# A GNN-attention-expert layer: the order of the expert routing, the distance of the second expert layer, and the last two tiles

## The chip, the cores and the metric

The kernel runs on one core of a Trainium2 chip. A core has a matrix engine (PE, with a separate queue for loading weights, PEld), a vector engine (DVE), a scalar engine (ACT), a general engine (POOL) and a queue engine (SP) that mostly starts DMA transfers. Each engine works through its own instructions in order and waits for the others by semaphores; ACT, SP and POOL also start transfers between the chip's memory (DRAM) and the on-chip memory. The metric is the device time of one execution in microseconds (us).

## The reference

One layer of a graph network over 1250 rows of 768 columns, in float32. A graph attention with two stages and a linear-attention mixer are added to `x`. What the change touches is the last part, a mixture of experts:

```python
logits = flat @ router_w.T                       # 1250 x 8
probs = jax.nn.softmax(logits, axis=-1)
topk_probs, topk_idx = jax.lax.top_k(probs, 2)
importance = probs.sum(axis=0)
running = 1 + 0.1 * (importance - 1) + 0.01
balanced = topk_probs / running[topk_idx]
balanced = balanced / balanced.sum(axis=-1, keepdims=True)
h = silu(einsum('th,eih->tei', flat, w1))        # 8 experts, 256 hidden
outs = einsum('tei,ehi->teh', h, w2)
x = x + sum over the two chosen experts of balanced * outs
```

`flat` is the normalised row. Each row thus goes to two of eight experts and gets back a weighted sum of two results.

## The kernel before

The rows are cut into ten tiles of 125 (`P`). The first 850 us hold the graph attention and the mixer and are not changed. The first five tiles of the updated rows are finished while the second attention layer of the other five still runs (`first_half`, L1131); there `stored` (L945) writes each finished row with its mean and reciprocal deviation (770 columns, `DX`) to two places in DRAM, `x2_d` and `xh_d`. The other five tiles are finished in the loop at L1242, and `stored(1)` writes them to `x2_d`.

**Expert tiles.** The kernel multiplies only what is chosen. It sorts the 2500 pairs of row and expert into tiles of 125 pairs that share one expert. The first 8 tiles, one for each expert, are filled from the first half of the rows and read `xh_d`; 16 more (`NQ1` = 24 in all) hold the rest and read `x2_d`. If the choice is uneven, a branch at the end computes up to nine further tiles; with these inputs it is not taken.

**Routing.** `placed` (L1048) ranks the logits, marks the two best and counts with two matmuls where each pair goes. `routed` (L1355) is a generator. Each call of `next(rt)` emits one portion of small DVE instructions and at times a list matmul on PE. A list is made by multiplying one-hot rows (`oh_r`) with values in bfloat16 pieces: `tokens` (L1301) makes the lists of row numbers, `roles` (L1323) the shares (weights), and for each pair the place of the row's other pair. The buffer `big` (5 x 770 columns) holds the one-hots during routing and gathered rows afterwards.

**The main loop** (L1478) has one step for each k from 0 to 23. For expert tile q:

- `gather(q)` (L1167) is an indirect DMA on POOL into one of 18 row buffers (`room`).
- `normed(q)` (L1176) normalises it, on ACT for the first eight tiles and on DVE for the others.
- `turned(q)` (L1189) transposes it on PE, and ACT copies it out of PSUM.
- `products(q)` (L1199) is the first expert layer, `gated(q)` (L1218) the silu, `hidden_turned(q)` (L1225) the transposition of the result.
- `halved(q)` (L1435) is the second expert layer: eight matmuls into `po`, then ACT scales by the share into `y`, SP stores `y` to `y_d` in DRAM and DVE adds it to the gathered row.
- `fetch_half(q)` (L1456) gathers by indirect DMA, for each pair of tile q, the result of the row's other pair if that one stands in an earlier tile. `hand_out(q)` (L1464) adds this half on DVE and scatters the finished rows to the output by another indirect DMA.

A row is written out by the later of its two tiles; for all others the index is out of bounds and the transfer leaves them out. All orders on PE, DVE, ACT and POOL are written out by hand here (`manual_schedule`), so each of these engines works in the order of the code. SP's order comes from a scheduler. Step k emits in this order:

```python
gated(k); turned(k + 2); next(rt, 0)
# one or two of halved(done), in part here and in part after products
normed(k + 3); products(k + 1); hidden_turned(k)
# POOL: hand_out(given), fetch_half(asked), then gather(got)
```

The constants at L1156 are `AHEAD` = 6 (how far gathers run ahead), `BEHIND` = 3 (buffers for fetched halves) and `LAG` = 6 (the first step with a `halved`). From step 6 on up to two `halved` go into a step, until the second layer is one tile behind the first; that is so from step 12 on. After the loop `halved(23)`, the remaining fetches and the remaining `hand_out` follow, each in turn.

Of the kernel before, what the change touches and what calls it, by code (L numbers as in the profile page):

```python
# [19 lines left out]
D = 768  # L20
# [49 lines left out]
def kernel(  # L70
# [874 lines left out]
    def stored(hf):  # L945

        t0, t1 = hf * TH_, (hf + 1) * TH_
        rs3 = rs3s[hf] = rstd_of(small, mv3, "c", t0, t1)
        nc.vector.tensor_copy(acc[:, t0:t1, D : D + 1], mv3[:, t0:t1, 0:1])
        nc.vector.tensor_copy(acc[:, t0:t1, D + 1 : DX], rs3.unsqueeze(2))  # L950
        for t in range(t0, t1):
            nc.sync.dma_start(out=x2_t[:, t, :], in_=acc[:, t, :DX])
            if not hf:
                nc.sync.dma_start(out=xh_t[:, t, :], in_=acc[:, t, :DX])
# [93 lines left out]
    def placed(psum, hf, pl):  # L1048
# [24 lines left out]
        pcum = psum.tile([P, 2, TH_, NE], F32, tag="rt" if hf else "tr", name=f"pcum_{hf}", bufs=1)  # L1073
# [12 lines left out]
        nc.vector.tensor_tensor(pos[:, hs], pcum[:, 0], cum, ALU.add)  # L1086
        picked(0, hs, pos[:, hs].unsqueeze(2).to_broadcast([P, TH_, 2, NE]), pick)
# [15 lines left out]

    def first_tiles(psum):
# [6 lines left out]
        pick0 = rtc.tile(two0, F32, name="pick0")  # L1111
# [44 lines left out]
    AHEAD, BEHIND, LAG = 6, 3, 6  # L1156
# [7 lines left out]
    room += [acc[:, t, :DX] for t in range(TH_, NT)] + [big[:, i * DX : (i + 1) * DX] for i in range(5)]  # L1164
    assert len(room) == 18
# [59 lines left out]
    def hidden_turned(q):  # L1225
        hT = exa.tile([128, 2, P], F32, tag="hT", name=f"hT_{q}", bufs=LAG + 1)

        def keep_h(b0, n, pt):
            if q < NE:
                nc.scalar.copy(hT, pt[:, :n, :])  # L1230
            else:
                nc.vector.tensor_copy(hT, pt[:, :n, :])  # L1232

        transposed(ps_x, hws.pop(q), [(0, 128), (128, 128)], keep_h, f"he{q}", bufs=3)
        hts[q] = hT
# [4 lines left out]
    plg = ps_x.tile([P, TH_, NE], F32, tag="rt", name="plg")  # L1240
    ft = first_tiles(ps_x)
    for i in range(TH_ + 3):  # L1242
# [8 lines left out]
        if 1 <= i <= TH_:  # L1251
            updated(ps_x, TH_ + i - 1)
# [22 lines left out]
    halves = exb.tile([P, BEHIND, D], F32, name="halves")  # L1275
    nc.gpsimd.memset(halves, 0.0)
# [24 lines left out]
    def tokens(oh, q0, q1):  # L1301
# [6 lines left out]
        plist = ps_x.tile([P, 2, w], F32, tag="rt", name=f"plist_{q0}")  # L1308
# [13 lines left out]

    def roles(oh, q0, q1, o, n):  # L1323


        w = q1 - q0
        more = carved(o, n * 2, 6, w)
        for i in range(3):
            listed(more[:, :, i, :], oh, parts[i][:, :n])
        listed(more[:, :, 3, :], oh, later[:, :n])  # L1330
        for i, v in ((4, q_), (5, r_)):
            for k in range(2):
# [3 lines left out]
                )  # L1336
        yield
        pmore = ps_x.tile([P, 6, w], F32, tag="rt", name=f"pmore_{q0}")
        for i in range(n * 2):
            nc.tensor.matmul(pmore, oh_r[:, i, :], more[:, i], start=(i == 0), stop=(i == n * 2 - 1))  # L1340
        lists = rtc.tile([P, 6, w], F32, tag="lists", name=f"lists_{q0}")
        nc.vector.tensor_copy(lists, pmore)
        nc.vector.tensor_tensor(share[:, q0:q1], lists[:, 1, :], lists[:, 2, :], ALU.add)
        nc.vector.tensor_tensor(share[:, q0:q1], share[:, q0:q1], lists[:, 0, :], ALU.add)
        goal = rtc.tile([P, 2, w], F32, tag="goal", name=f"goal_{q0}")
        nc.vector.scalar_tensor_tensor(
            goal[:, 0, :], lists[:, 4, :], float(P), lists[:, 5, :], op0=ALU.mult, op1=ALU.add
# [3 lines left out]
            goal, goal, -BIG, lists[:, 3:4, :].to_broadcast([P, 2, w]), op0=ALU.add, op1=ALU.mult  # L1351
        )
        nc.vector.tensor_scalar(take[:, 1:3, q0:q1], goal, BIG, None, op0=ALU.add)

    def routed():  # L1355


        pl = placed(ps_x, 1, plg)
        next(pl)
        yield  # L1360
        for _ in pl:
# [11 lines left out]
        nc.vector.tensor_tensor(q_[:, TH_:], nth[:, TH_:], at[:, 1, TH_:], ALU.add)  # L1373
        rows_of(1)
# [6 lines left out]

        def each(v):
            return v.unsqueeze(2).to_broadcast([P, NT, NE])

        nc.vector.tensor_reduce(red[:, 1, :], prob, AX.X, ALU.add)
        nc.vector.reciprocal(red[:, 2, :], red[:, 1, :])
        nc.vector.tensor_tensor(prob, prob, each(red[:, 2, :]), ALU.mult)

        imp = rtc.tile([P, NE], F32, name="imp")
        nc.vector.tensor_reduce(imp, prob.rearrange("p t e -> p e t"), AX.X, ALU.add)  # L1390
# [3 lines left out]
        pim = ps_x.tile([P, NE], F32, tag="rt", name="pim")  # L1394
        nc.tensor.matmul(pim, ones[:P, :P], imp, start=True, stop=True)
        nc.vector.tensor_scalar(used, end[0:1, NE - 1 : NE], 1.0, None, op0=ALU.add)

# [4 lines left out]
        run = rtc.tile([P, NE], F32, name="run")  # L1402
        nc.vector.tensor_scalar(run, pim, 1.0, 1.0 - 0.9, op0=ALU.subtract, op1=ALU.mult)
        nc.vector.tensor_scalar(run, run, 1.0, 0.01, op0=ALU.add, op1=ALU.add)
        rrun = rtc.tile([P, NE], F32, name="rrun")
        nc.vector.reciprocal(rrun, run)
        nc.vector.tensor_tensor(prob, prob, rrun.unsqueeze(1).to_broadcast([P, NT, NE]), ALU.mult)
        yield
        comb = lg
        nc.vector.tensor_tensor(comb, sel, prob, ALU.mult)  # L1410
        nc.vector.tensor_reduce(red[:, 3, :], comb, AX.X, ALU.add)
        nc.vector.reciprocal(red[:, 3, :], red[:, 3, :])
        nc.vector.tensor_tensor(comb, comb, each(red[:, 3, :]), ALU.mult)
        picked(2, slice(0, NT), comb.unsqueeze(2).to_broadcast(two), pick)

        rest = at[:, 2]
        for i in range(3):
            nc.vector.tensor_copy(parts[i], rest)
            if i < 2:
                nxt = rtc.tile([P, NT, 2], F32, name=f"rest_{i}")  # L1420
                nc.vector.tensor_tensor(nxt, rest, parts[i], ALU.subtract)
                rest = nxt
        yield
        oh_a = carved(6180, TH_, 2, NE)
        told(oh_a, 0, NE)
        first_ones = roles(oh_a, 0, NE, 2500, TH_)
        next(first_ones)
        yield
        for _ in first_ones:
            pass  # L1430
        yield
        for _ in roles(oh_b, NE, NQ1, 2980, NT):
            yield

    def halved(q, keep=True):  # L1435
# [17 lines left out]
        nc.vector.tensor_tensor(xg[:, :D], xg[:, :D], y, ALU.add)  # L1453
        sums[q] = xg[:, :D]

    def fetch_half(q):  # L1456
        if q > 0:
            nc.gpsimd.indirect_dma_start(  # L1458
                out=halves[:, q % BEHIND, :], out_offset=None, in_=y_d[0 : q * P, :],
                in_offset=bass.IndirectOffsetOnAxis(ap=take[:, 1, q : q + 1], axis=0),  # L1460
                bounds_check=q * P - 1, oob_is_err=False,
            )

    def hand_out(q):  # L1464
        fin = sums.pop(q)
        if q > 0:
            nc.vector.tensor_tensor(fin, fin, halves[:, q % BEHIND, :], ALU.add)
# [10 lines left out]
    for k in range(NQ1):  # L1478
        gated(k)
        if k + 2 < NQ1:  # L1480
            turned(k + 2)
        next(rt, 0)
        n = min(2, k - done) if k >= LAG else 0
        if k == NQ1 - 1:
            n = 1
# [3 lines left out]
        if k + 3 < NQ1:  # L1489
            normed(k + 3)  # L1490
        if k + 1 < NQ1:
            products(k + 1)
# [3 lines left out]
        hidden_turned(k)  # L1496
        while asked < done - 1:
# [5 lines left out]
        if given == 0 < done:  # L1503
# [3 lines left out]
        while k >= 3 and got < min(given + len(room), k + 1 + AHEAD, NQ1 if k >= 8 else len(room) - 5):  # L1507
            gather(got)
            got += 1
    halved(NQ1 - 1, keep=False)  # L1510
    assert done == NQ1 - 1
# [80 lines left out]
```

## Time and profile before

| | us |
|---|---|
| median of 3 runs | 1088.83 (1085.12 to 1092.47) |
| the profiled execution | 1084.71 |
| its span | 1082.9 |
| PE busy | 989.9 (91%) |
| DVE busy | 646.6 (60%) |
| ACT busy | 388.2 (36%) |
| POOL busy | 159.9 (15%) |
| first expert product starts | 884.4 |
| last matmul ends | 1055.2 |

The span is the time from the first to the last instruction of the profiled execution. Rows of the profile name the line of the code, the operation, the output and its inputs, and the duration. `ph` is the output of `products`, `po` that of `halved`, `tr_xe` that of `turned`, `tr_he` that of `hidden_turned`. `x_d` is `x2_d`. [...] In square brackets stands the idle time of the engine before the row, and what ended it.

### The profile page before, as it was taken

To read this page: it belongs to the slowest core of one execution; us is meant where nothing else is said; L and a number is where in the kernel's file an instruction comes from. 1 tells how busy PE (TensorE), PEld (TensorE's weight loads), DVE (VectorE), ACT (ScalarE), POOL (GpSimd) and SP (SyncE) were. 2 spreads that over 40 slices of the span, in tenths; PEclk is the share of its full clock that TensorE was granted. 3 is DMA by queue.
4 is the path that set the end of the run, shared out by engine and by line. 5 is a ranking of instruction groups with operands and counts; after the bars stand their busy time and mean duration, and the time that the engine had idled before them with its cause. 6 is when DMAs were issued, how large, how long until landed. Compare 5 with 4: busy or idle time off the path is not lost. (4 is left out here: it accounts for less than half of the span.)

```text
span 1082.9 us, 13295 instructions
## 1 busy us (share of the span) xinstructions
PE 989.9 (91%) x4893; PEld 754.6 (70%) x4893; DVE 646.6 (60%) x1411; ACT 388.2 (36%) x697; POOL 159.9 (15%) x157
## 2 busy tenths in 40 slices
PE   5988999999997999999999999999999788999980
PEld 4877888874574558989889875567778577766750
DVE  7338974441845835776675984946677655444542
ACT  0244422330000007646556750045457344332320
POOL 1000000000000000000000011432210031256543
PEclk9998999999998999999999999999999899999995
DMA  8400000031232101000002232221062268255443
GB/s 209 139 29 4 16 23 22 13 111 71 75 118 91 54 24 42 15 24 24 24 23 89 84 131 96 86 75 52 25 212 85 97 197 271 85 167 176 149 119 101
DMA packets 55429, 93.26 MB, mean 86 GB/s; under 512 B 22705, under 2 KB 29041, under 8 KB 55355
## 3 DMA queue, kind: packets, MB, share of 16 engines
q1 hardware_dynamic: 30966, 73.63, 20.0%
q0 software_dynamic: 15904, 17.02, 5.7%
q10 hardware_dynamic: 8484, 1.65, 0.8%
q8 instruction: 43, 0.70, 0.3%
q14 instruction: 32, 0.25, 0.1%
HBM read 75.53 MB, written 27.04 MB: 95 GB/s over the span
## 5 line engine op out<-in xcount | busy, mean ns | idle before, releaser
L777 PE MATMUL pa_a<-acc,p_a 125*125 125x197 f32 x800 | 144.6, 333 | 1.1 <-DVE p_a L773 0.7
L777 PEld LDWEIGHTS pa_a<-acc,p_a 125*125 125x125 f32 x800 | 133.7, 187 | 12.6 <-issue 5.8
L773 DVE SCALAR_TENSOR_TENSOR p_a<-e_a,cntT 125x625 f32<-125x625 f32 x80 | 64.5, 816 | 40.9 <-PE pa_a L777 39.8
L642 PE MATMUL pg<-W,xnT 128*125 128x396 f32 x240 | 82.5, 507 | 6.0 <-DVE acc L645 6.0
L337 DVE TENSOR_SCALAR ohd<-iota,dst_f 125x125 bf16<-125x125 int16 (+1 forms) x170 | 50.5, 297 | 61.4 <-PE pe L344 61.4
L849 PE MATMUL po<-wu_sb,xnT 128*125 128x384 f32 x240 | 82.0, 490 | 5.4 <-ACT acc L853 4.1
L483 PE MATMUL pk_k<-xnT,wk_sb 128*128 128x250 f32 x360 | 83.2, 374 | 0.0
L483 PE MATMUL pk_q<-xnT,wq_sb 128*128 128x250 f32 x360 | 80.0, 375 | 2.7 <-PEq L695 1.9
L771 DVE SCALAR_TENSOR_TENSOR e_a<-e_a,e_a 125x625 f32<-125x625 f32 x80 | 65.9, 835 | 25.6 <-ACT e_a L767 13.9
L483 PEld LDWEIGHTS pk_q<-xnT,wq_sb 128*128 128x128 f32 x360 | 67.2, 189 | 12.0 <-issue 3.3
L769 ACT ACTIVATE e_a<-rowt_a,s1x 125x625 f32<-125x625 f32 x80 | 64.5, 817 | 30.7 <-DVE e_a L771 30.5
L642 PEld LDWEIGHTS pg<-W,xnT 128*125 128x125 f32 x240 | 45.9, 192 | 42.0 <-DVE acc L645 6.7
L767 ACT ACTIVATE e_a<-rowt_a,s 125x625 f32<-125x625 f32 x80 | 64.6, 815 | 28.4 <-DVE p_a L773 27.0
L1441 PE MATMUL po<-ew,hT 128*125 (+1 forms) x192 | 68.7, 502 | 5.5 <-DVE hT L1232 5.0
L483 PEld LDWEIGHTS pk_k<-xnT,wk_sb 128*128 128x128 f32 x360 | 66.9, 189 | 6.8
L459 DVE CUSTOM_DVE_ANT_0 junk<-nmr,rows 125x1250 f32<-125x1250 bf16 x40 | 58.3, 1457 | 19.9 <-DMA rows<-sr_d 14.4
L1212 PE MATMUL ph<-ew,xTe 128*125 (+1 forms) x288 | 69.3, 392 | 0.0
L849 PEld LDWEIGHTS po<-wu_sb,xnT 128*125 128x125 f32 x240 | 43.6, 188 | 36.0 <-ACT acc L853 6.7
L333 DVE TENSOR_SCALAR ohs<-iota,smod,wgt 125x417 bf16<-125x417 int16 x170 | 65.4, 385 | 0.0
L1212 PEld LDWEIGHTS ph<-ew,xTe 128*125 128x125 f32 x288 | 55.6, 195 | 12.0
L344 PE MATMUL pe<-ohs,ohd 125*125 125x418 bf16 x206 | 55.4, 369 | 9.2 <-DVE ohd L337 8.5
L777 PEld LDWEIGHTS pa_b<-h,p_b 125*125 125x125 f32 x400 | 49.2, 193 | 8.7 <-DVE p_b L773 2.8
(344 smaller groups left out, 1591.0 us busy)
## 6 DMA issues: line engine op xcount, KB each, us to landing
y_d<-y SPq DMA_DIRECT2D x23, 375.0 KB
ew<-in_w1T SPq DMA_DIRECT2D x8, 768.0 KB
ew<-in_w2T SPq DMA_DIRECT2D x8, 768.0 KB
nmr<-nm_d SPq DMA_DIRECT2D x20, 305.2 KB
rowt_a<-ab_d SPq DMA_DIRECT2D x8, 610.4 KB
x_d<-acc SPq DMA_DIRECT2D x10, 376.0 KB
acc<-in_x SPq DMA_DIRECT2D x10, 375.0 KB
xr<-in_x SPq DMA_DIRECT2D x10, 375.0 KB
```

The lines of the kernel that those rows point to most:

```text
L333: nc.vector.tensor_scalar(oh_s[:, :TH], iota[:, :TH], smod[:, c : c + 1], wgt[:, c : c + 1], op0=ALU.is_equal, op1=ALU.mult)
L459: nc.vector.tensor_tensor_reduce(out=junk, in0=nm, in1=row, scale=1.0, scalar=-3.0e38, op0=ALU.add, op1=ALU.max, accum_out=mx_col)
L483: nc.tensor.matmul(pk[:, i, :], w_sb[:, k, f * 128 : (f + 1) * 128], xnT[:, k, g * GN : (g + 1) * GN], start=(k == 0), stop=(k == KD - 1),)
L642: nc.tensor.matmul(pg, xnT[:, k, t * P : (t + 1) * P], W12[:, k, cs], start=(k == 0), stop=(k == KD - 1))
L767: nc.scalar.activation(e1, rowt[:, 0, :], AF.Exp, bias=s[:, h, 0, u : u + 1])
L769: nc.scalar.activation(e2, rowt[:, 1, :], AF.Exp, bias=sx[:, h, u : u + 1])
L771: nc.vector.scalar_tensor_tensor(e1, e1, 1.0, e2, op0=ALU.min, op1=ALU.max)
L773: nc.vector.scalar_tensor_tensor(p, e1, 1.0, cntT[:, u, hf * HN : (hf + 1) * HN], op0=ALU.min, op1=ALU.mult)
L777: nc.tensor.matmul(pas[i][:, :cw], p[:, i * P : (i + 1) * P], hv, start=(u == 0), stop=(u == NT - 1))
L849: nc.tensor.matmul(po[:, hf, :384], xnT[:, k, ts], wu_sb[:, k, cs], start=(k == 0), stop=False)
L1212: nc.tensor.matmul(ph, xT[:, k, :], ew1[:, whose_r[q], k, :].rearrange("p o i -> p (o i)"), start=(k == 0), stop=(k == KD - 1),)
L1441: nc.tensor.matmul(po[:, hf, :384], hT[:, c, :], ew2[:, e_r, c, hf * 384 : (hf + 1) * 384].rearrange("p o n -> p (o n)"), start=(c == 0), ...
```

## The change

**Stores.** In the first half all stores to `xh_d` go ahead of those to `x2_d`. In the second half each tile's 768 columns are stored when the tile is done, and mean and deviation of all five tiles follow in one transfer of two columns.

**Routing.** The balanced weights are computed ahead of the lists. A new `first_shares` makes the shares of the first eight tiles from `pick0`, directly after. Two portions of `routed` are emitted in each step, one before and one after the matmuls. All small PSUM results share one bank, `prt`, each at its own columns. `roles` makes three lists for the first tiles instead of six. The routing ends in step 6 and not in step 8.

**Loop.** `LAG` is 3, so `halved` starts in step 3 and is one tile behind from step 6 on. The tiles under 8 are normalised ahead of the routing portion. Fetches start at step 7 and have six buffers, two of them parts of `big`; `room` has 16. Gathers of tiles 8 to 12 start at step 4, those from 13 on at step 9 (before: 3 and 8).

**Last two tiles.** Fetches for tiles 22 and 23 read only the results of tiles 0 to 20. For a row whose other pair stands in tile 21 or 22, a one-hot matrix (`chosen`, in steps 10 to 12) picks the result from SBUF by a matmul (`crossed`). The last `halved` adds with one DVE instruction from PSUM.

The core of the diff:

```diff
-        for t in range(t0, t1):
-            nc.sync.dma_start(out=x2_t[:, t, :], in_=acc[:, t, :DX])
-            if not hf:
-                nc.sync.dma_start(out=xh_t[:, t, :], in_=acc[:, t, :DX])
+        if hf:
+            nc.sync.dma_start(out=x2_t[:, t0:t1, D:DX], in_=acc[:, t0:t1, D:DX])
+        else:
+            for to in (xh_t, x2_t):
+                for t in range(t0, t1):
+                    nc.sync.dma_start(out=to[:, t, :], in_=acc[:, t, :DX])
...
-    AHEAD, BEHIND, LAG = 6, 3, 6
+    AHEAD, BEHIND, LAG = 6, 6, 3
+    LATE = 2
...
-            updated(ps_x, TH_ + i - 1)
+            t = TH_ + i - 1
+            updated(ps_x, t)
+            nc.sync.dma_start(out=x2_t[:, t, :D], in_=acc[:, t, :D])
...
+    halves = [halves_t[:, i, :] for i in range(BEHIND - 2)]
+    halves[2:2] = [big[:, i * DX : i * DX + D] for i in (3, 4)]
+    PAIRS = [(q, f) for q in range(NQ1 - LATE, NQ1) for f in range(NQ1 - LATE - 1, q)]
...
+    def first_shares():
+        more = carved(6340, TH_ * 2, 3, NE)
+        for i in range(3):
+            listed(more[:, :, i, :], pick0, parts[i][:, :TH_])
+        yield
+        psh = prt[:, 136:160].rearrange("p (i q) -> p i q", i=3)
+        for i in range(TH_ * 2):
+            nc.tensor.matmul(psh, oh_r[:, i, :], more[:, i], start=(i == 0), stop=(i == TH_ * 2 - 1))
+        three_l = rtc.tile([P, 3, NE], F32, name="three_l")
+        nc.vector.tensor_copy(three_l, psh)
+        nc.vector.tensor_tensor(share[:, :NE], three_l[:, 1, :], three_l[:, 2, :], ALU.add)
+        nc.vector.tensor_tensor(share[:, :NE], share[:, :NE], three_l[:, 0, :], ALU.add)
...
+    def chosen(j):
+        oh = exa.tile([P, P], F32, tag="chosen", name=f"chosen_{j}", bufs=1)
+        nc.vector.tensor_scalar(oh, col, which[:, j : j + 1], None, op0=ALU.is_equal)
+        pt = ps_x.tile([128, 4, P], F32, tag="tr", name=f"tr_ch{j}", bufs=3)
+        nc.tensor.transpose(pt[:P, 0, :], oh, ident[:P, :P])
+        nc.scalar.copy(chosenT[:, j, :], pt[:P, 0, :])
+
+    def crossed(q):
+        fs = [(j, f) for j, (q2, f) in enumerate(PAIRS) if q2 == q]
+        for hf in range(2):
+            px = ps_x.tile([128, 4, P], F32, tag="tr", name=f"px_{q}_{hf}", bufs=3)
+            px = px.rearrange("p a b -> p (a b)")[:P, :384]
+            for n, (j, f) in enumerate(fs):
+                nc.tensor.matmul(
+                    px, chosenT[:, j, :], kept[f][:, hf * 384 : (hf + 1) * 384],
+                    start=(n == 0), stop=(n == len(fs) - 1),
+                )
+            cs = slice(hf * 384, (hf + 1) * 384)
+            to = (sums[q] if q in sums else xgs[q])[:, cs]
+            nc.vector.tensor_tensor(to, to, px, ALU.add)
...
-        nc.vector.tensor_tensor(xg[:, :D], xg[:, :D], y, ALU.add)
+        if keep:
+            nc.vector.tensor_tensor(xg[:, :D], xg[:, :D], y, ALU.add)
+        else:
+            xa = xg[:, :D].rearrange("p (a c) -> p a c", a=2)
+            nc.vector.scalar_tensor_tensor(
+                xa, po[:, :, :384], share[:, q : q + 1], xa, op0=ALU.mult, op1=ALU.add
+            )
...
-    for k in range(NQ1):
+    LISTS, ROLES = 4, 7
+    for k in range(NQ1 - 1):
         gated(k)
         if k + 2 < NQ1:
             turned(k + 2)
+        if k + 3 < NE:
+            normed(k + 3)
         next(rt, 0)
         n = min(2, k - done) if k >= LAG else 0
-        if k == NQ1 - 1:
-            n = 1
         if n and k > LAG:
             halved(done)
             done, n = done + 1, n - 1
-        if k + 3 < NQ1:
+        if NE <= k + 3 < NQ1:
             normed(k + 3)
-        if k + 1 < NQ1:
-            products(k + 1)
+        if k == NQ1 - 2:
+            hidden_turned(k)
+            halved(done)
+            done += 1
+        products(k + 1)
         if n:
             halved(done)
             done += 1
-        hidden_turned(k)
-        while asked < done - 1:
+        next(rt, 0)
+        if k != NQ1 - 2:
+            hidden_turned(k)
+        if 10 <= k < 10 + len(PAIRS):
+            chosen(k - 10)
+        while k >= ROLES and asked < min(done - 1, NQ1 - LATE - 1):
             if asked - given == BEHIND:
                 hand_out(given)
                 given += 1
             fetch_half(asked)
             asked += 1
-        if given == 0 < done:
+        while k >= ROLES and (given == 0 < done or (k > NQ1 - 6 and given < asked - 2)):
             hand_out(given)
             given += 1
-        while k >= 3 and got < min(given + len(room), k + 1 + AHEAD, NQ1 if k >= 8 else len(room) - 5):
+        while k >= LISTS and got < min(given + len(room), k + 1 + AHEAD, NQ1 if k >= 9 else len(room) - 3):
             gather(got)
             got += 1
-    halved(NQ1 - 1, keep=False)
-    assert done == NQ1 - 1
+    while asked - given > 2:
+        hand_out(given)
+        given += 1
+    nc.gpsimd.memset(halves_t[:, 2:4, :], 0.0)
+    for q in range(asked, NQ1):
+        fetch_half(q)
+    q = NQ1 - 1
+    gated(q)
+    crossed(q - 1)
+    hand_out(given)
+    hidden_turned(q)
+    crossed(q)
+    hand_out(given + 1)
+    halved(q, keep=False)
+    given += 2
     while given < NQ1:
-        if asked < NQ1 and asked - given < BEHIND:
-            fetch_half(asked)
-            asked += 1
-        if asked < NQ1 and asked - given < BEHIND:
-            continue
         final = hand_out(given)
         given += 1
```

## The prediction

> **What bounds the kernel now.** I read the page first, then the busy time by stage, then the order of single instructions in the expert stage, then the chain that ended last. All that the change touches begins near 858 us, and nearly all of it after 884 us, where the first expert tile is multiplied. Two rows of the page are used below (the second, for ACT's queue: packets, MB, share of 16 engines' span):
>
> ```profile
> span 1082.9 us, 13295 instructions
> ...
> q10 hardware_dynamic: 8484, 1.65, 0.8%
> ```
>
> The stages after 884 us (length, then the busy time of PE, PEld, DVE, ACT, POOL, granted clock, DMA share, GB/s):
>
> ```profile
> 884.00:954.00 70.00, 64.02 (x330) 49.83 (x329) 33.96 (x121) 28.77 (x57) 14.04 (x11) 0.95 0.58 182
> 972.00:990.00 18.00, 14.51 (x60) 9.96 (x59) 8.26 (x13) 5.07 (x10) 13.14 (x10) 0.91 0.65 192
> 990.00:1040.00 50.00, 49.28 (x222) 36.14 (x221) 24.98 (x39) 16.67 (x31) 28.79 (x21) 1.00 0.46 142
> 1055.20:1082.90 27.70, 0.00 (x0) 0.00 (x0) 5.67 (x6) 0.90 (x1) 9.78 (x8) 0.54 0.35 103
> ```
>
> From 990 to 1040 PE has 49.28 of 50 us: the steady steps are PE's. In the 70 us of the ramp (routing and the first tiles) PE idles 6 us, in 972 to 990 it idles 3.5, and after 1055.2 it has nothing for 27.7 us. One steady step of the loop, from the order of instructions, PE and then POOL:
>
> ```profile
> 1027.45 0.38 PE L146 MATMUL tr_he<-ident,hw 125*128 125x125 f32 x2
> 1027.69 0.83 PE L146 MATMUL tr_xe<-ident,xme 125*128 125x125 f32 x6
> 1028.43 2.82 PE L1441 MATMUL po<-ew,hT 128*125 x8
> 1031.08 2.75 PE L1212 MATMUL ph<-ew,xTe 128*125 x12
> 1033.67 0.38 PE L146 MATMUL tr_he<-ident,hw 125*128 125x125 f32 x2
> ```
>
> ```profile
> 1029.47 1.23 POOL L1468 DMA_INDIRECT out<-big,take  x1 [3.42 <-DVE big L1467]
> 1031.00 1.29 POOL L1458 DMA_INDIRECT halves<-y_d,take  x1 [0.30 <-issue]
> ```
>
> A step is the hidden transposes `he(k)` (`hidden_turned`), `turned(k+3)`, `halved(k)`, `products(k+2)`; the next `he` is at 1033.67, so 6.22 us, with no idle of PE. On POOL the `out` goes 2.02 us after `he`, for its DVE add stands behind the copy of `he`; the fetch of a half goes at 3.55 and the next gather at 5.1 (1020.14 after the `he` of 1015.00). POOL at the end:
>
> ```profile
> 1061.42 1.23 POOL L1468 DMA_INDIRECT out<-acc,take  x1 [0.30 <-issue]
> 1062.95 1.38 POOL L1458 DMA_INDIRECT halves<-y_d,take  x1 [0.30 <-issue]
> 1064.64 1.23 POOL L1468 DMA_INDIRECT out<-acc,take  x1 [0.30 <-issue]
> 1067.77 1.22 POOL L1468 DMA_INDIRECT out<-acc,take  x1 [1.91 <-DVE acc L1467]
> 1071.51 1.20 POOL L1468 DMA_INDIRECT out<-spare,take  x1 [2.52 <-DVE spare L1467]
> ```
>
> After the last product POOL and the landings are the chain: `out`, fetch, 7.2 us to land, an add on DVE of 0.96 at 1070.26, the last `out`, and 11.4 us from its issue to 1082.9.
>
> **The change, part by part.** I follow `he(k)`, the end of step k.
>
> *Ramp, steps 0 to 6.* The new order is one tile behind from step 6 on; before it is so only from step 12. The `normed` of the first tiles now precedes the routing on DVE, which takes away ACT's late normalisations: PE waited 7.9 us for them in five places (the waits of this stage); three of the five, 1.78 + 2.15 + 1.45 = 5.4 us, go. In their place come waits of PE for lists. In three slots the list's matmuls stand directly behind `turned`, and the DVE work that they need was queued behind an add that waits for the last `halved`. Take step 4: po ends, ACT's `y` 0.15 + 0.90, the add 0.96, the comparison and two lists 1.43 (900.76 to 902.19), in all 3.5 us; beside it PE has only `he` and `turned`, 0.87. So 2.6 us there, 2.6 at step 5 by the same sum, and 2.3 at step 2, where the shares' list waits for DVE (its chain from 889.28, with the rows of before: 899.7; PE is there at 897.4). PE's work from 884.37 to `he(6)`: the first product 4.05, seven at 2.6, seven `turned` at 0.64, seven `he` at 0.22, six `halved` at 2.6 (start to start in the chain), list matmuls 4.3 (0.38 + 0.53 + 0.54 + 1.13 + 0.54 + 1.14 in before): 48.1 us; with 7.5 us for lists and 1.4 in small waits `he(6)` is at 941.4. Three steps on, `he(9)` is at 960.0 with 9 halves done; `he(11)` would be at 972.5 with 11. Before has `he(11)` at 971.54 with 11. The ramp thus gives nothing: +1.0. The second-layer weights load in time: their first use is near 906 and not 922.9, but 1.9 MB of stores no longer stand ahead of them (882.05 to 887.2).
>
> *Stores.* Five stores of whole rows become five of 768 columns, earlier, and one of two columns: 625 runs of 8 bytes. The nearest row is ACT's queue of small packets: 0.8% of 16 engines' 1083 us over 8484 packets is 16 ns each, so 625 take 10 us of one engine. [...]
>
> *Gathers.* This is the term that decides. Tile 13 is gathered in step 9 (`k >= 9`; before in step 8), and in POOL's order it stands behind `hand_out(1)` and `fetch_half(7)`. The `out` of tile 1 waits for a DVE add behind the copy of `he(9)`. So POOL stands idle for some 10 us and gather 13 issues at `he(9)` + 5.1 = 965.1. Gathers of that place took:
>
> ```profile
> L1170 POOL DMA_INDIRECT big<-x_d,take x5: 1214/1227/1883, 946.7 to 984.1; - x5
> ...
> DMA to landing us min/median/max: 7.9/10.4/12.5
> ```
>
> With 10 us it lands at 975.1. `normed(13)` is on DVE in step 10, ahead of the copy of `he(10)` and the new comparison of `chosen(0)`: 0.7 + 0.4 + 0.2, then PE has one transpose and `turned(13)` at 976.8, where it was due at 966.5 (`he(10)` + 0.24). Queued behind on DVE: the copy, the comparison, `out(2)`; on PE: everything. +10.3; ends: 8 with a landing of 7.9, 13 with 12.5. From then on gather k+6 leaves at `he(k)` + 5.1 and is wanted at `he(k+3)`, as before.
>
> *Clock.* After a gap the clock can be low:
>
> ```profile
> 899.91 0.86 PE L146 MATMUL tr_xe<-ident,xme 125*128 125x125 f32 x6 [2.15 <-ACT xme L1182]
> 900.61 4.44 PE L1212 MATMUL ph<-ew,xTe 128*125 128x256 f32 x12
> ```
>
> This product took 4.44 us behind a 2.15 us gap; at full clock 2.76. [...] But 2.24 us of idle at 1050 to 1052 left the next po at 2.82, so I take +1.7.
>
> *Steady steps 11 to 21.* Before lost 6.2 us there against 10 x 6.22, 5.5 of it in 972 to 990, where adds waited for halves fetched late. With six halves in flight this goes: -6.2. `chosen` adds two more PE transposes with their order, +0.5; five adds at step 19 (4.8 us of DVE) delay `normed(23)` by about 1.1. So `he(21)`: 976.8 + 6.0 + 1.7 + 62.2 + 0.5 + 1.1 = 1048.3; before 1039.90.
>
> *End.* From `he(21)` the order po(21), `he(22)`, po(22) is what before does one step later: po(22) ends at +9.07, the tile's add at +11.0, `out(18)` at +12.2. Then a memset of 1536 columns (1.4, from 2.04 for 2304), three fetches at +15.2, +16.8, +18.4 (1.29 and 0.30 each), landing 7.2, add 1.0, `out` at +26.85, 11.4 to the end: +38.25. Before: 1082.9 - 1039.9 = 43.0. The matmuls of `crossed` (six of 0.7 us) and po(23) end at +19.3 and the last fused sum at +20.4: hidden under the landing; without that cover they would cost 4.2. Gain 4.75.
>
> *Sum.* 1048.3 + 38.25 = 1086.5 against a span of 1082.9: +3.6 us. The profiled execution took 1084.71; the median of the runs is 1088.83 (1085.12 to 1092.47), so 1092.
>
> **Rivals.** *Gathers in time*: if POOL reaches gather 13 a step earlier, or `out(1)` does not hold it, the 10.3 and 1.7 go: -8.4, 1080. For it: before has the same gathers go straight behind a fetch (946.67). Against: in the steady step every `out` waits for its add. *Cold clock*: all three list gaps pay 1.7 each and the gathers land in 13 us, as at 994.5 to 1007.8: 3.6 + 5.1 + 3 = +11.7, 1100.5, slower. It decides from three cold gaps on; with one it stays within 1%. *The end on PE*: if the three last fetches land before po(23) ends, DVE goes straight from the fused sum (+20.4) through three adds (2.9) to the last `out` (+23.5) and the end is at +34.9 instead of +38.25: 1089. Against: they leave at +15.2 to +18.4, and none of before landed in under 6 us.
>
> **How the numbers follow.** A measurement of this kernel tells about 1% (11 us) from no change. The forecast, with the end on PE in it, 0.55 (1085 to 1099); gathers in time 0.19 (1074 to 1085); cold clock or another late transfer 0.26 (1097 to 1110). The range from 1077 leaves out about 0.08 below and to 1104 about 0.1 above. Faster by over 1% needs the gathers in time and 2.5 us more: 0.14; slower takes most of the cold case and a little of the forecast: 0.26.
>
> **What would show it.** PE idle in one piece of 8 to 13 us near 966 to 977, ended by tile 13's normalisation, POOL idle before `out(1)`; list matmuls waiting 2 to 3 us at steps 2, 4, 5; no losses from 980 to 1040; after the last matmul about 19 us, ended by the fetch of tile 23. Wrong would be: no piece over 3 us after `he(9)`; the lists' DVE work faster than my queue sums; or a second late transfer.

## The result: 1% slower than before

The changed kernel took 1098.9 us in the median (1096.55 to 1103.24, 8 runs), the kernel before 1090.05 (1085.12 to 1098.81, 8 runs beside it). The ratio is 1.011, with a 95% interval of 1.008 to 1.014. The ratios, here and below, leave out single runs over 1.5% above the fastest of their kernel and need not equal the quotient of the medians (1.008 here). The prediction was 1092, about no change, in a range of 1077 to 1104. The time lies in the range; the kernel is slower by about 1%, and the interval leaves out no change.

The profiled execution of the changed kernel has a span of 1096.0 us against 1082.9. A row of its page, and the first gather that reads `x2_d`:

```profile
span 1096.0 us, 13377 instructions
...
917.55 1.23 POOL L1178 DMA_INDIRECT acc<-x_d,take  x1 [38.31 <-DVE used L1467]
```

This gather was released by DVE's routing (`used`) and not by the 625 short stores. The stages of the changed kernel (length, then the busy time of PE, PEld, DVE, ACT, POOL, granted clock, DMA share, GB/s):

```profile
888.00:951.00 63.00, 56.07 (x294) 43.26 (x293) 32.13 (x120) 26.74 (x50) 12.09 (x10) 0.95 0.55 177
951.00:969.00 18.00, 18.00 (x83) 13.27 (x82) 6.87 (x12) 6.56 (x13) 6.20 (x6) 1.00 0.35 112
969.00:987.00 18.00, 6.67 (x21) 4.49 (x21) 2.67 (x6) 1.40 (x4) 7.42 (x6) 0.62 0.39 109
1002.00:1052.00 50.00, 49.49 (x225) 36.38 (x224) 28.62 (x44) 16.77 (x33) 32.08 (x23) 1.00 0.51 152
1074.50:1096.00 21.50, 0.03 (x1) 0.00 (x0) 3.89 (x4) 0.90 (x1) 8.08 (x7) 0.59 0.33 93
```

The ramp (888 to 951) is idle on PE for 6.9 of 63 us. From 951 to 969 PE has no gap at all. From 969 to 987 it works for 6.7 of 18 us, and that stretch was not in the kernel before. The steady steps are as full as before (49.49 of 50), and from 1074.5 on PE is done for 21.5 us. Steps of the loop look as they did, PE first and then POOL, from the order of instructions:

```profile
1022.74 0.38 PE L146 MATMUL tr_he<-ident,hw 125*128 125x125 f32 x2
...
1028.96 0.38 PE L146 MATMUL tr_he<-ident,hw 125*128 125x125 f32 x2
```

```profile
1024.74 1.23 POOL L1548 DMA_INDIRECT out<-acc,take  x1 [1.42 <-DVE acc L1547]
```

A step is still 6.22 us, from `he` at 1022.74 to `he` at 1028.96, and the `out` still leaves 2.0 us after `he`.

The long gap, on POOL, on PE and in the view of the gathers' source line (time from issue to landing; POOL's rows for these gathers last 1.2 to 1.7 us):

```profile
965.46 1.23 POOL L1548 DMA_INDIRECT out<-acc,take  x1 [10.59 <-DVE acc L1547]
966.99 1.28 POOL L1537 DMA_INDIRECT halves<-y_d,take  x1 [0.30 <-issue]
968.58 1.69 POOL L1178 DMA_INDIRECT big<-x_d,take  x1 [0.30 <-issue]
```

```profile
963.46 0.38 PE L146 MATMUL tr_he<-ident,hw 125*128 125x125 f32 x2
...
981.39 0.54 PE L1488 MATMUL tr_ch<-ident,chosen 125*125 125x125 f32 x1 [11.33 <-DVE chosen L1486]
981.72 1.46 PE L146 MATMUL tr_xe<-ident,xme 125*128 125x125 f32 x6
982.97 4.34 PE L1512 MATMUL po<-ew,hT 128*125 x8
```

```profile
L1178 POOL DMA_INDIRECT big<-x_d,take x3: 1207/1217/1692, 968.6 to 972.1; - x3
...
  DVE xme L1192: 10.9, 1
...
DMA to landing us min/median/max: 8.3/9.5/11.3
```

POOL stood idle for 10.59 us in front of the `out` of tile 1, whose DVE addition waits for step 9. Behind it in POOL's order came a fetch and only then the gather of tile 13, issued at 968.58, which is `he(9)` (963.46) + 5.1. The three gathers issued there landed within 8.3 to 11.3 us, and that of tile 13 was the slow one: its normalisation, for which DVE waited 10.9 us, began 11.5 us after the issue (980.04). The comparison of `chosen(0)` stood behind that, and PE stood idle for 11.33 us. The next product then ran at a low granted clock (0.63 from 983.0 to 987.3), 4.34 us instead of 2.82.

POOL at the end:

```profile
1068.22 1.22 POOL L1548 DMA_INDIRECT out<-acc,take  x1 [6.36 <-DVE acc L1547]
1069.43 1.42 POOL L1603 MEMSET halves<- 125x1536 f32 x1
1071.04 1.30 POOL L1537 DMA_INDIRECT big<-y_d,take  x1 [0.19 <-issue]
1072.65 1.91 POOL L1537 DMA_INDIRECT halves<-y_d,take  x1 [0.30 <-issue]
1074.87 1.27 POOL L1537 DMA_INDIRECT halves<-y_d,take  x1 [0.30 <-issue]
...
1081.68 1.92 POOL L1548 DMA_INDIRECT out<-spare,take  x1 [0.99 <-DVE spare L1547]
1083.90 1.19 POOL L1548 DMA_INDIRECT out<-spare,take  x1 [0.30 <-issue]
```

After `out` at 1068.22 come the memset, three fetches and five scatters. The last scatter leaves at 1083.90, and the execution ends 12.1 us later.

**Where the 13.1 us of span came from.** I set the working of the prediction beside the two traces, stage by stage:

| us | predicted | measured |
|---|---|---|
| first product | 884.4 | 888.2 |
| to `he(9)` | 75.6 | 75.3 |
| `he(9)` to `turned(13)` | 16.8 | 18.3 |
| to `he(11)` | 7.7 | 8.0 |
| `he(11)` to `he(21)` | 63.8 | 64.6 |
| `he(21)` to the end | 38.25 | 41.6 |
| span | 1086.5 | 1096.0 |

Before had 87.2 to `he(11)` (now 101.6), 68.4 from there to `he(21)` (now 64.6) and 43.0 to the end (now 41.6). So the stretch to `he(11)` costs 14.4, the steady steps give some 3.7 back and the end 1.4. The first product came 3.8 us later, in code that the change does not touch on PE, DVE and ACT in its order. It need not be an effect of the change: in the experiments below the first product starts between 883.9 and 892.0 (once at 899.6), and 892.0 is a kernel with the order of before. I therefore compare times counted from the first product, and the medians.

### The profile page after: what moved, and what is told of

The parts are those of the page before. It is cut to its first block, busy times and chain, and to the rows that moved or that the text cites. A ratio compares the mean times of both kernels' runs of the same rounds, so it can differ in the third digit from the quotient of the medians.

```text
span 1096.0 us, 13377 instructions
## 1 busy us (share of the span) xinstructions
PE 999.2 (91%) x4918; PEld 762.0 (70%) x4918; DVE 647.9 (59%) x1421; ACT 388.9 (35%) x700; POOL 161.8 (15%) x158
## 5 line engine op out<-in xcount | busy, mean ns | idle before, releaser
L773 DVE SCALAR_TENSOR_TENSOR p_a<-e_a,cntT 125x625 f32<-125x625 f32 x80 | 63.3, 801 | 40.9 <-PE pa_a L777 39.8
L1512 PE MATMUL po<-ew,hT 128*125 (+1 forms) x192 | 72.0, 521 | 3.2 <-DVE hT L1240 2.8
L767 ACT ACTIVATE e_a<-rowt_a,s 125x625 f32<-125x625 f32 x80 | 64.6, 815 | 27.5 <-DVE p_a L773 26.1
```

What stands on the lines that cost most here:

```text
L767: nc.scalar.activation(e1, rowt[:, 0, :], AF.Exp, bias=s[:, h, 0, u : u + 1])
L773: nc.vector.scalar_tensor_tensor(p, e1, 1.0, cntT[:, u, hf * HN : (hf + 1) * HN], op0=ALU.min, op1=ALU.mult)
L1512: nc.tensor.matmul(po[:, hf, :384], hT[:, c, :], ew2[:, e_r, c, hf * 384 : (hf + 1) * 384].rearrange("p o n -> p (o n)"), start=(c == 0), ...
```

## The experiments

My theory: three things cost the change its gain, each for itself. (1) The gather of tile 13 stands behind a scatter on POOL that waits, because it is let go at step 9. (2) The list matmuls stand on PE ahead of DVE work that is not done. (3) The last fetches leave late, behind the `out` of tile 18. The rival to (1) is that the landing itself, or the order of lists, is what is late, so that an earlier issue only moves the wait. The rival to the whole is that these gaps cover one another, so that taking one away brings up the next.

### Gathers from step 8

```diff
-        while k >= LISTS and got < min(..., NQ1 if k >= 9 else len(room) - 3):
+        while k >= LISTS and got < min(..., NQ1 if k >= 8 else len(room) - 3):
```

> The changed kernel with one number altered: tiles from 13 on may be gathered from step 8 and not from step 9. Queue theory: gather 13 then stands behind the fetch of tile 6 (953.6 in the changed kernel) and not behind the write-out of tile 1 (965.5), so it issues near 955 and lands near 965, before its normalisation is due. The gap of 11.3 us and the slow stretch after it (1.6) go: span 1096.0 - 12.9 = 1083, ratio to the kernel before 0.997 to 1.002. Rival, the transfer is late by itself (contention of the gathers with stores and fetches): the gap stays over 5 us, ratio 1.005 to 1.011.

Measured: 1085.08 us, ratio 0.998 (0.995 to 1.001). POOL, then PE, at the place of the gap:

```profile
961.62 1.22 POOL L1178 DMA_INDIRECT big<-x_d,take  x1 [0.30 <-issue]
963.15 1.22 POOL L1178 DMA_INDIRECT big<-x_d,take  x1 [0.31 <-issue]
971.89 1.23 POOL L1548 DMA_INDIRECT out<-acc,take  x1 [7.53 <-DVE acc L1547]
```

```profile
977.29 0.34 PE L1488 MATMUL tr_ch<-ident,chosen 125*125 125x125 f32 x1 [0.80 <-DVE chosen L1486]
```

Gather 13 is now the first of the two at 961.62 and 963.15 (step 8 lets 13 and 14 go), ahead of the scatter that waits until 971.89 for its addition. The 11.33 us gap is gone; 0.80 us are left, for DVE's comparison. `he(11)` is at +92.7 after the first product, against +101.6, although this execution lost 4 us more in the ramp than the changed kernel's (`he(4)` at +39.8 and not +35.8, a low clock behind the 2.46 us gap for the list of step 4: the product there took 5.41 us instead of 2.82).

### Gathers ahead of the scatters in the same step

```diff
+        while k >= LISTS and got < min(..., NQ1 if k >= 9 else len(room) - 3):
+            gather(got)
+            got += 1
         while k >= ROLES and (given == 0 < done or ...):
             hand_out(given)
             given += 1
-        while k >= LISTS and got < min(..., NQ1 if k >= 9 else len(room) - 3):
-            gather(got)
-            got += 1
```

> The changed kernel with the gathers still from step 9 on, but in every step ahead of write-outs and fetches in POOL's order. Queue theory: it is the place in POOL's order that costs, not the step, so the gap goes as with the earlier step: gather 13 near 955, span about 1083, ratio 0.997 to 1.002; later gathers leave 3 us earlier in each step, which gives nothing more because PE sets those steps. Rival, the step number itself or the load on the transfers decides: the gap stays, ratio 1.005 to 1.011.

Measured: 1084.94 us, ratio 0.9968 (0.995 to 0.9986). POOL, with gather 13 first:

```profile
958.95 1.23 POOL L1178 DMA_INDIRECT big<-x_d,take  x1 [0.30 <-issue]
...
969.23 1.23 POOL L1548 DMA_INDIRECT out<-acc,take  x1 [6.01 <-DVE acc L1547]
```

The gap is gone here too, `he(11)` at +91.8. The step is the same as in the changed kernel, only the place in POOL's queue is another. That is cause (1) shown: what stood ahead of the gather made the gap, and the landing alone does not.

### The late gather put into the kernel before

```diff
-        while k >= 3 and got < min(..., NQ1 if k >= 8 else len(room) - 5):
+        while k >= 3 and got < min(..., NQ1 if k >= 9 else len(room) - 5):
```

> The kernel before with its last gathers let go a step later (9 instead of 8), nothing else. By the theory of the POOL queue, the gather of tile 13 is then put behind a scatter that waits for VectorE here as well, and tile 11 or 12's product waits 4 to 10 us for it: ratio 1.004 to 1.009. If the wait belongs to the changed kernel's order of lists and not to the step from which the gathers are let go, nothing changes: 0.998 to 1.002.

Measured: 1103.24 us, ratio 1.013 (1.008 to 1.018), 14 us for one number. POOL and PE of this kernel:

```profile
964.44 1.66 POOL L1468 DMA_INDIRECT out<-acc,take  x1 [10.21 <-DVE acc L1467]
...
971.34 1.22 POOL L1170 DMA_INDIRECT big<-x_d,take  x1 [0.30 <-issue]
```

```profile
969.85 0.38 PE L146 MATMUL tr_he<-ident,hw 125*128 125x125 f32 x2
981.22 1.51 PE L146 MATMUL tr_xe<-ident,xme 125*128 125x125 f32 x6 [10.99 <-DVE xme L1184]
```

The same picture in the old order of lists and lag: a scatter that waits 10.21 us, gathers behind it, PE idle 10.99 us for tile 13's normalisation. `he(11)` comes at +99.4 instead of +87.2. So the loss needs neither the new lists nor the crossing. It was more than the 4 to 10 us I had expected, for here two scatters and two fetches stand ahead of the gather, which leaves at `he(9)` + 10.5.

### The lists' DVE work ahead of the second product

```diff
         if k + 3 < NE:
             normed(k + 3)
         next(rt, 0)
         n = min(2, k - done) if k >= LAG else 0
+        next(rt, 0)
         if n and k > LAG:
             halved(done)
...
             halved(done)
             done += 1
-        next(rt, 0)
```

> The changed kernel with the second routing portion of a step emitted ahead of the second half of second-layer products and not behind it, so that its DVE work no longer waits for that add. Queue theory: the waits of the list matmuls at steps 4 and 5 (2.46 and 2.10 us) go and the slow stretch at 927.6 (1.7) with them, the one at step 2 (1.98) stays; from the first expert product to the hidden transposes of step 6 it takes 51 to 52.5 us and not 56.8; the later gap stays as long as it is. Ratio 1.004 to 1.008. Rival, DVE as a whole is too slow for the routing: the waits move to the next list, 56 us, ratio 1.010.

Measured: 1089.19 us, ratio 1.001 (0.999 to 1.003), and `he(6)` at +50.4 instead of +56.8. The list matmuls of steps 4 and 5:

```profile
912.72 1.28 PE L1327 MATMUL prt<-big 125*125 125x32 bf16 x20
...
922.54 0.70 PE L1374 MATMUL prt<-big 125*125 125x24 bf16 x10
```

They run without a wait, where the changed kernel had 2.46 and 2.10 us. Together that is 4.6 us; the other 1.8 of the 6.4 is nearly all the low clock behind such a gap. In the changed kernel, at steps 4 and 5:

```profile
914.97 1.27 PE L1327 MATMUL prt<-big 125*125 125x32 bf16 x20 [2.46 <-DVE big L1314]
...
927.05 0.75 PE L1374 MATMUL prt<-big 125*125 125x24 bf16 x10 [2.10 <-DVE big L1362]
927.64 4.52 PE L1512 MATMUL po<-ew,hT 128*125 128x384 f32 x8
```

The product behind the 2.10 us gap took 4.52 us and not 2.83, at a granted clock of 0.62. The long gap, ahead of the transposes of step 11, stayed at 11.23 us. That is cause (2). The ratio fell below the 1.004 to 1.008 expected: the time gained some 10 us, the trace 6.4. A likely reason, which no run isolates: of the five profiles that have the list gap of step 4, two kept the full clock behind it (`he(6)` at +56.8) and three did not (+60.0 to +60.9).

### The last fetches ahead

```diff
+        if k == NQ1 - 2:
+            nc.gpsimd.memset(halves_t[:, 2:4, :], 0.0)
+            for q in range(asked, NQ1):
+                fetch_half(q)
         while k >= ROLES and (given == 0 < done or ...):
             hand_out(given)
...
-    nc.gpsimd.memset(halves_t[:, 2:4, :], 0.0)
-    for q in range(asked, NQ1):
-        fetch_half(q)
```

> The changed kernel with the memset and the last three fetches of halves ahead of the write-out of tile 18 in POOL's order (which waits 6.4 us for its add at 1068.2). Queue theory: the fetches leave near 1064 to 1067 and not 1071 to 1075, and land before the last products are added, so the end is set by PE and three adds: last write-out near 1079.7 and not 1083.9, span -4 us, ratio 1.006 to 1.008. Rival, the products and the crossing matmuls set the end already: 0 to -1 us, ratio 1.010.

Measured: 1096.27 us, ratio 1.010 (1.007 to 1.013): no gain that shows, and the ratio that the rival had. POOL of this kernel at the end:

```profile
1062.23 1.56 POOL L1537 DMA_INDIRECT halves<-y_d,take  x1 [0.30 <-issue]
...
1076.71 1.19 POOL L1548 DMA_INDIRECT out<-spare,take  x1 [0.30 <-issue]
```

The last fetch leaves at 1062.23, which is `he(21)` + 12.3 instead of + 20.5, and PE and DVE become the bound of the end. The last scatter leaves 2.8 us earlier (+26.7, was +29.5). But 13.1 us follow it and not 12.1. So of the 4 us I expected 1.8 were left in the trace: cause (3) was there, it was small, and the time does not show it. In its place came what follows the scatters.

### Without the crossing

```diff
-        n = q if q < NQ1 - LATE or q >= NQ1 else NQ1 - LATE - 1
+        n = q
...
-        if 10 <= k < 10 + len(PAIRS):
-            chosen(k - 10)
...
-    nc.gpsimd.memset(halves_t[:, 2:4, :], 0.0)
-    for q in range(asked, NQ1):
+    for q in range(asked, NQ1 - 1):
         fetch_half(q)
...
-    crossed(q - 1)
     hand_out(given)
     hidden_turned(q)
-    crossed(q)
     hand_out(given + 1)
+    fetch_half(q)
```

> The lists' order and the lag of the change as they are, the crossing taken out: the last two tiles' halves are fetched from the stored list of outputs as in the kernel before. The crossing is worth little by theory A: without it 4.2 us of TensorE work, 2 us of gaps at the three matrices and the memset go, and the last fetch leaves about when it does in the changed kernel (1074.9 there), because it waits for POOL and not for the store of the last output; then the end is he(21)+41 +- 2 and the ratio to before 1.007 to 1.011. By theory B the crossing does save the wait for the store and its landing: then the last scatter goes out 6 to 8 us later, the end is he(21)+47 to +49, and the ratio 1.013 to 1.018.

Measured: 1097.33 us, ratio 1.008 (1.006 to 1.010), as theory A said. From `he(11)` to `he(21)` it takes 62.75 us instead of 64.6, and the end 42.5 instead of 41.6. The two nearly cancel: as it stands in the change, the crossing is worth nothing that these runs can tell.

### The three edits together, and the transposes split

The first kernel holds the edits of the gathers (step 8), the lists and the fetches. The second has also this, so that PE meets each comparison a step after DVE made it:

```diff
-        oh = exa.tile([P, P], F32, tag="chosen", name=f"chosen_{j}", bufs=1)
+        oh = exa.tile([P, P], F32, tag="chosen", name=f"chosen_{j}", bufs=2)
         nc.vector.tensor_scalar(oh, col, which[:, j : j + 1], None, op0=ALU.is_equal)
+        yield
         pt = ps_x.tile(...)
...
+        if 11 <= k <= 10 + len(PAIRS):
+            for _ in ch:
+                pass
         if 10 <= k < 10 + len(PAIRS):
-            chosen(k - 10)
+            ch = chosen(k - 10)
+            next(ch)
```

> The three edits that were tried one by one, together: gathers from step 8 instead of 9, the lists' half step ahead of the second product, the last fetches ahead of the end. If each cause is its own (theory A), the gains add: about -12 (gather) -9 (lists, on the time to before: 1.0108 to 1.0013 is -10) -1 to -2 (end), so 1075 to 1078 us, ratio 0.987 to 0.990. By theory B, the tiles come round to the same transfers once a gap is gone (the gather issued at step 8 is needed 6 us earlier than in the run with that edit alone), so half of it or more comes back as a wait at steps 11 to 13: 1082 to 1086, ratio 0.994 to 0.998.

> As the three edits together, and the three matrices' transposes one step behind their comparisons on VectorE. If the 0.8 us gaps at these (1.6 to 2.4 us in all) are the wait for VectorE's comparison, they go, and the time is 1.5 to 2.5 us under that of the three edits together. If the gap only moves to the next wait for VectorE, it is the same within 0.5 us.

The three together: 1077.42 us, the median of four with the profiled execution of 1089.17; the ratio, from the other three, is 0.989 (0.985 to 0.994). The single edits moved the ratio by -0.0128, -0.0095 and -0.0006 from 1.0108; their sum would be 0.988. So the causes add within that interval, and its profile has no new wait over 1 us. (That execution is 11 us late before the first product, so I read only its stages: `he(21)` at +148.2, was +166.2.)

With the transposes split: 1069.84 us, ratio 0.985 (0.980 to 0.990). The stages of this kernel from the end of the ramp, with the columns as above:

```profile
950.00:968.00 18.00, 18.00 (x81) 13.14 (x80) 8.47 (x15) 6.01 (x11) 7.65 (x6) 1.00 0.52 164
968.00:1031.00 63.00, 62.31 (x284) 45.95 (x283) 35.13 (x56) 21.62 (x43) 41.46 (x31) 1.00 0.52 152
```

PE has 18.00 of 18 us in the stretch in which the changed kernel stood still, and 62.3 of 63 in the steady steps. From `he(10)` to `he(21)` it takes 69.3 us; with the three edits alone 71.8, as in both kernels with only the gathers moved. The 2.5 us is at the upper end of what I expected of the split (1.5 to 2.5). The times of the two kernels differ by more, 7.6 us, but their intervals overlap, so the times show no size for it.

### Again, and without the crossing

The same kernel with more executions, and the three edits with the crossing taken out as above. There the fetch of tile 23 goes between the `out` of tile 19 and that of tile 20, and no transposes are needed.

> The kernel with the three edits and the split transposes once more, with more executions, next to the one without the crossing: 0.985 to the kernel before (0.982 to 0.987).

> The three edits together as before, and the crossing taken out of that kernel: the halves of tiles 21 and 22 fetched ahead of the end from the stored list, that of tile 23 after the store of output 22; no matrices, so their gaps are gone too. By theory A (the crossing was worth nothing only because POOL was busy and waiting until 1074.9 anyway) it does pay once the fetches lie ahead: the last fetch now waits for the store of output 22, at he(21)+18 to +20 instead of +12, and the last scatter goes out 4 to 6 us later, against 2.4 us of gaps and steps saved: 1072 to 1076 us, 2 to 5 over the kernel with the split transposes, ratio 0.987 to 0.991. By theory B (the crossing is worth nothing here either, the end is set by the additions and the twelve us after the last scatter) it is no slower than the kernel with the split transposes: 0.983 to 0.986.

Measured: with the crossing 1072.08 us, ratio 0.986 (0.981 to 0.990), so the gain stands; without it 1075.97, ratio 0.989 (0.984 to 0.993). POOL, then PE, of the kernel without the crossing:

```profile
1054.06 1.29 POOL L1537 DMA_INDIRECT halves<-y_d,take  x1 [1.48 <-SPq L1620]
...
1062.35 1.19 POOL L1548 DMA_INDIRECT out<-spare,take  x1 [2.21 <-DVE spare L1547]
```

```profile
1041.07 4.51 PE L1512 MATMUL po<-ew,hT 128*125 x8 [2.24 <-DVE hT L1240]
```

The fetch waits for SP's store and leaves at 1054.06, `he(21)` + 19.2, as theory A said (+18 to +20). The last scatter leaves at +27.5, only 2.5 us later than with the crossing (+25.1 in both of its profiles). Of that 1.7 is the low clock of the product at 1041.07, which took 4.51 us and in both profiles with the crossing 2.82. Not all of the difference is the end: from `he(11)` to `he(21)` this kernel took 64.4 us and the two with the crossing 62.9 and 63.1, for PE waited three times for a normalisation (0.72, 0.99 and 0.51 us); whether that comes of the edit is open. The times differ by 3.9 us with overlapping intervals. That the crossing pays once the fetches lie ahead is likely and not shown.

## Why the prediction was right, and where its sum was short

**The gathers** were the term that decides, and it was as described: POOL idle before `out(1)` for 10.59 us ("some 10"), gather 13 at `he(9)` + 5.1 to the tenth, the landing 8.3 to 11.3 (10 taken). To `turned(13)` it was 18.3 and not 16.8 us, since gather 13 landed at the upper end. Removing the order on POOL removed the gap, and putting it into the kernel before made it. Tested in two ways, this step is shown.

**Ramp.** `he(9)` was forecast 75.6 us after the first product and came at 75.3; the list gaps were 1.98, 2.46 and 2.10, forecast 2.3, 2.6 and 2.6. That the ramp gives nothing holds. The close match is partly luck: with the same ramp, three other profiles have `he(9)` at +78.4 to +79.3, as the clock stayed low behind the gap of step 4. The edit of the lists shows that the ramp could have given 6.4.

**Stores** have no term in the sum: the gather that needs them waited 38.31 us for DVE and not for them, which agrees. No run took them apart, and none shows what a run of 8 bytes takes; the 10 us of one engine was an estimate from ACT's queue.

**Clock.** I took 1.7 us, behind the long gap alone. That it falls there and not behind the list gaps was my estimate, which no run of before showed and the runs do not bear out: what came is 1.5 behind the long gap (4.34 for 2.82), 1.7 behind the list gap of step 5 and 1.7 behind the gap of 2.24 us at 1058 to 1060. Here I had chosen by a row of before, where a gap of that length left the next product at 2.82. One row was too little to choose by, as the last section shows. The cold clock as a rival was right for one of three list gaps in this profile, and for two of three in three other profiles (4.97 to 5.41 us at step 4, 4.17 to 4.52 at step 5).

**Steady steps.** Forecast -6.2 against before, +0.5 for `chosen`, +1.1 for five additions. The kernel without the crossing, which has no `chosen`, needs 62.75 us where before needed 68.4, so -5.6 for the first and the third, against -5.1. `chosen` cost about 1.9 and not 0.5: to its transposes came 0.80 us of PE's wait for DVE each time, which I had seen as order and not as a wait. That the -6.2 comes from six halves in flight was argued, and no run took it apart.

**End.** This is the term that was mis-sized: a gain of 4.75 was forecast, 1.4 came. The working gave 38.25 after `he(21)`, measured are 41.6. Of the 3.4 us, 1.7 is the cold second product of tile 22, which put `out(18)` at +13.9 instead of +12.2. About 0.4 more is the second fetch, 1.91 us instead of 1.29, less some 0.2 saved before it. From the last fetch to the last scatter it took 9.0 and not 8.45, for the scatter of tile 22 took 1.92 and held POOL. And 12.1 us followed the last scatter, not 11.4, for it landed after 6.8 and not 6.1 us. None of these is a new mechanism; all are small terms that I had taken at their best row.

So the order of events was right, and the sum was 5.7 us short: 1.5 us at the gathers, 1.1 after it, 3.4 at the end, less 0.3 at the ramp. That put the time some 1% above before and not within 1% of it. The rest of the difference to the forecast span, 3.8 us, is the start, which varies by as much between the profiles.

**Rivals.** *Gathers in time* was put at 1080; the kernels in which they are in time took 1085: in both their profiles the end took 40.9 to 41.9 us and not 38.25, and the ramp lost 3 to 4 us more behind the gap of step 4. *The end on PE* is what the two kernels with the split show: after the fused sum DVE goes straight on, and the last scatter leaves at +25.1 (forecast +23.5). But the end came at +38.1 and +37.7 instead of +34.9. The first of the two:

```profile
1052.69 1.64 POOL L1549 DMA_INDIRECT out<-spare,take  x1 [1.50 <-DVE spare L1548]
1054.63 1.19 POOL L1549 DMA_INDIRECT out<-spare,take  x1 [0.30 <-DVEq L1629]
1056.13 1.19 POOL L1549 DMA_INDIRECT out<-spare,take  x1 [0.30 <-issue]
```

The last three scatters leave within 3.4 us of one another, and 13.1 us follow the last.

## What to carry to other kernels

On POOL, which took its orders in turn in these runs, a transfer was let go by what is queued ahead of it and not only by the step in which it is written. One gather that stands behind a scatter waiting for another engine cost 11 to 14 us here, and moving the gathers ahead of the scatters gave them back. When a change rearranges a loop, look for the first PE instruction of each step whose input comes from DVE, and put the DVE work at least one product ahead of it: the lists and the three transposes gave 6.4 and 2.5 us so. And with the end on DMA, count what follows the last transfer as part of the sum, since it is not fixed (11.3 to 13.1 us here).

## What the runs showed of the hardware

**The same gap of 2.24 us left the clock low in nine of twelve profiles.** Every kernel has it before the second-layer product of tile 22. After it the product took 4.51 us in the changed kernel and 4.22 to 4.51 in eight of the others, and 2.82 in the kernel before and in the two profiles with the split transposes. The changed kernel, then the first with the split:

```profile
1060.61 4.51 PE L1512 MATMUL po<-ew,hT 128*125 x8 [2.24 <-DVE hT L1240]
```

```profile
1037.31 2.82 PE L1513 MATMUL po<-ew,hT 128*125 x8 [2.24 <-DVE hT L1240]
```

The granted clock during the first of these two was 0.62; during the same product of the kernel before, also 2.82 us, it was 1.00. The other gaps near 2 us were as little of one kind. After 1.97 to 1.99 us (step 2) the product ran at full clock in nine profiles of ten and took 4.21 us in one (the execution of 1089.17 us). After 2.10 to 2.11 us (step 5) it was slow in five of five (4.17 to 4.52 us). After 2.46 us (step 4) it was at full clock in two profiles and took 4.97 to 5.41 us in three. So 2.0 to 2.5 us of idle can leave the clock low, and do not always. For a sum of this kernel, a gap of 2 us or more should be priced as a range: from its length alone to 1.7 us more, and 3.3 more at the worst seen here, where the list matmuls behind the gap took 2.02 us instead of 1.27 and the product 5.41 instead of 2.82.

**What follows the last scatter is not fixed.** In these twelve profiles it goes with how close the last ones are. Where the last three leave within 6.9 to 7.3 us, 11.3 to 11.4 us follow the last one (the kernel before, the late gather in it, the first kernel without the crossing). Within 3.5 to 4.9 us it is 11.75 to 12.3, and within 3.4 us 12.65 to 13.1 (the four kernels with the fetches ahead and the crossing). So kernels that brought the last scatters together gave back up to 1.7 us. What differs is the landing of the last scatter: in the eight profiles that show it, the execution ends 5.2 to 5.3 us after that landing. The view of the last scatter in the kernel before, then in the first with the split:

```profile
L1468 POOL DMA_INDIRECT out<-spare,take x1: 1197/1197/1197, 1071.5 to 1071.5; - x1
...
DMA to landing us min/median/max: 6.1/6.1/6.1
```

```profile
L1549 POOL DMA_INDIRECT out<-spare,take x1: 1189/1189/1189, 1056.1 to 1056.1; - x1
...
DMA to landing us min/median/max: 7.8/7.8/7.8
```

It landed after 6.0 to 6.1 us in the three kernels with the widest spacing, after 6.5 and 6.8 in two between, and after 7.4 to 7.8 in three of the closest. The step from 12.0 at 3.5 to 12.65 at 3.4 is too sharp for the spacing alone; what else sets the landing was not tried.
